# Products of weights and group-norm statistics made beside the scans of a Mamba layer, in a four-layer kernel

## The chip, the core and the metric

The kernel runs on one core of a Trainium2 chip, as one program. The metric is the device time in microseconds (us) of one execution; lower is better. The core has a matrix engine (TensorE, PE in the profile, with its weight loads as PEld), a vector engine (VectorE, DVE), a scalar engine for activations (ScalarE, ACT), a general engine (GpSimd, POOL) and a queue engine that issues nearly all transfers here (SyncE, SP). Each works through its own list of instructions in order; semaphores hold an instruction until what it reads is written and what it overwrites has been read. SBUF is the on-chip memory with 128 partitions (`P`), PSUM the memory that PE writes, in banks of 512 float32 values per partition. DRAM is outside.

## What is computed

Input is `x`, 2 images of 256 channels and 48 x 48 points (`NB` = 2, `C` = 256, `L` = 2304 points), float32. Four layers follow each other:

```python
x = _L0_conv_ref(x, ...)                       # layer 0: Mamba, forward and backward
x = x + _L1_conv_ref(_gn(x), ...)              # layer 1: linear attention, 3x3 conv, MLP
t = _to_tokens(x)
t = t + _L2_attn_ref(_ln_t(t), W_embed, b_embed, W_out, b_out)   # layer 2
t = t + _L2_ffn_ref(_ln_t(t), ...)             # experts gated by a graph
t = t + _L3_attn_ref(_ln_t(t), q_weight)       # layer 3
t = t + _L3_ffn_ref(_ln_t(t), ...)             # mixture of experts
```

Three pieces of it bear on the change.

The group norm between layers 0 and 1, over groups of 8 channels and all points of an image:

```python
g = v.reshape(B_, G, C_ // G, H_, W_)
m = jnp.mean(g, axis=(2, 3, 4), keepdims=True)
s = jnp.var(g, axis=(2, 3, 4), keepdims=True)
return ((g - m) / jnp.sqrt(s + eps)).reshape(v.shape)
```

The scans of layer 0: for every channel of 512 and each of 16 states, h(t) = exp(dt A) h(t-1) + dt u B, y = sum over states of h C, once forward and once backward over the points.

The attention of layer 2, three heads, in which queries, keys and values are consecutive thirds of the points and the head's matrix `W` (768 x 256) and bias `b` serve all three:

```python
e = jnp.einsum('bmc,hc->bmh', x, W) + b
q, k, v = jnp.split(e, 3, axis=1)
attn = jax.nn.softmax(jnp.einsum('bmd,bnd->bmn', q, k) * SCALE, axis=-1)
return jnp.einsum('bmn,bnd->bmd', attn, v)
```

The heads' outputs are concatenated along the points and multiplied by `W_out` (256 x 768), and `b_out` is added.

## The kernel before

The state of the network stays in SBUF between layers: `xres` (residual stream, 128 partitions x 2 halves of the channels x 4608 points) and `xn` (its normalised form). Points are handled in pieces of `W` = 384; an image has `NCH` = 6 pieces. The program is written as Python functions with generators; a scheduler then orders the instructions of each engine, and derives the semaphores from the tiles. Tiles come from pools; a tag with `bufs` = n has n buffers in turn, and a new tile waits until the old content of its buffer has been used.

**Layer 0** (L130 to L434) runs 24 scans, in the order batch, forward then backward, piece (list `order`, L405). In this text a scan's index counts them from 0. One scan covers one piece of 384 points and has 4 blocks of channels x 16 states = 64 operations. Each operation is: an exponential on ACT (L376), a scan instruction on DVE (L382 forward, L385 backward), a product with C on DVE or POOL (L390, tile `hc`; 40 of the 64 on DVE, 24 on POOL), and a product with the identity on PE that sums into `yp` (L344). POOL also makes the products dt u B (`db`, L359, four states at a time). B and C rows are loaded by SP, spread over all partitions (`bb`, `cc`), four states at a time, from two buffers each.

Beside a scan, other work is advanced in small steps: `scan` takes a list `beside` of (generator, number of steps, end) and, after every second operation, calls the generators so that their steps are spread evenly until slot `end` of 32 (L395 to L399). Beside go `project_out` of the scan before (2 steps, backward scans only; it adds into `xres`), `prepare` of the next scan (15 steps: convolution L266, projections L282 and L296, several activations), and, in scans 0 to 9, `project_in` of a later piece (12 steps; layer norm L176 to L195 and 8 products of two matmuls, L202, each copied by ACT and stored by SP). All this work takes its PSUM tile from `hold()`: while scans run, that is one bank, pool `ps` with one buffer, tag "mm". The other PSUM banks hold the exponentials (pool `psh`, five) and `yp` (two). `prepare`'s products are therefore made and evicted one at a time. `pos`, `h`, `sq` and `rs` are single-buffered tiles of `project_in`.

At the start of layer 0 SP loads the small constants, the first piece of `xres`, the projection weights `w_in` (1 MB, L154), the position table, and the other pieces of `xres`.

**Layer 1** (L459 to L675) first loads its weights, makes two block matrices with `same_block` (`gmat`, which averages over groups of 8 channels, and `hmask`), clears the padded image `img` on POOL (L500), and calls `group_norm(0)`: 12 `bn_stats`, two aggregates, a product with `gmat` that averages the means over a group (L520), some small operations, a second one for the variances (L528), root and reciprocal, then `xn` = (x - mean) / sigma in two instructions (L533). Then come keys and values (`pk`, L547), which read `xn`. `group_norm(1)` is called within batch 0's pieces. A part of the sort of the graph's edges (helpers around L880 to L910) is spread over layer 1 and reaches into layer 2.

**Layer 2's attention** (L680 to L816) uses that W embeds queries and keys alike: q k' = x (W' W) x', and the values' path is `W_out` W. Both products depend on weights alone. For each of three heads, `W_embed[h]` and `W_outT` are loaded side by side into `w_eo` (two transfers of 768 KB, L708 and L709), and `gm[h]` = W'[W, W_out'] is made in two blocks of 128 rows, each of six matmuls 128x512 (L713), copied by DVE (L717). The bias terms `ub` are matmuls with one column (L721), 24 per head. Then, per batch, `xv` is made by transposing `xn` (L741, L742), and for each head queries `pq` (L750) from `gm` and `xn`, scores `sp` (L764), softmax, output and the residual.

The records of float32 matmuls in the profile come in pairs: one matmul of the program is two records.

Of the kernel before, what the change touches and what calls it, by code (L numbers as in the profile page):

```python
# [52 lines left out]
class Env:  # L53


    def __init__(self, ctx, tc, p):
# [16 lines left out]
        self.xres = const.tile([P, 2, T], F32, name="xres")  # L73

    def uid(self):
        self.n_pools += 1
        return self.n_pools
# [37 lines left out]
def run(steps):  # L115
    for _ in steps:
        pass


# [9 lines left out]
def layer0(ctx, E):  # L129
# [33 lines left out]
    def hold():  # L163

        pool, tag = (ps, "mm") if scanning else (psh, "hs")
        return pool.tile([P, W], F32, tag=tag, name="mm")

    def project_in(b, c):
# [13 lines left out]
        for k in range(2):  # L182
            nc.tensor.matmul(vp, lhsT=E.mean_c, rhs=sq[:, k, :], start=k == 0, stop=k == 1)
        rs = up.tile([P, W], F32, tag="rs", name="rs")
        nc.scalar.activation(rs, vp, AF.Sqrt, bias=E.eps[1e-5])
# [132 lines left out]
    def project_out(b, c, y):  # L318

        for m in range(2):  # L320
# [8 lines left out]
            yield  # L329

    def scan(step, beside, b, s, c, xs, y, dt, dtu, bcd):

# [19 lines left out]
        for d0, g in [(d0, g) for d0 in range(0, DB, 2) for g in range(NS // GN)]:  # L352
# [4 lines left out]
            for d in (d0, d0 + 1):  # L357
# [14 lines left out]
                for j in range(GN):  # L372
                    n = g * GN + j
                    on_pool = j in GP[(g + d) % 2]
                    hs = psh.tile([P, W], F32, tag="hs", name="hs")
                    nc.scalar.activation(  # L376
# [46 lines left out]
    pieces = [(0, c) for c in range(2, NCH)] + [(1, c) for c in range(NCH)]  # L423
    after = None
    for i, (b, s, step, c) in enumerate(order):
        now, ready = ready, []
        beside = [(after, 2, 5)] if after else []
        if i + 1 < len(order):
            nb, s2, _, c2 = order[i + 1]
            beside.append((prepare(nb, s2, c2, ready), 15, 25))  # L430
        if i < len(pieces):
            beside.append((project_in(*pieces[i]), 12, 32))
        scan(step, beside, *now)
        after = project_out(b, c, now[4]) if s == "b" else None  # L434
# [25 lines left out]
def layer1(ctx, E, edges):  # L460
# [20 lines left out]

    gmat = big.tile([P, P], F32, name="gmat")
    same_block(E, lw, gmat, 3, 1.0 / 8)
    hmask = big.tile([P, P], F32, name="hmask")
# [25 lines left out]
    def group_norm(b):  # L510

        xb = E.xres[:, :, b * L : (b + 1) * L]
        mv = wp.tile([P, 2, 2], F32, tag="mv", name="mv")
        for k in range(2):
            st = wp.tile([P, NCH, 6], F32, tag="st", name="st")
            for c in range(NCH):
                nc.vector.bn_stats(st[:, c, :], xb[:, k, c * W : (c + 1) * W])
            nc.vector.bn_aggr(mv[:, k, :], st)
        pg = ps.tile([P, 2], F32, tag="mm", name="pg")
        nc.tensor.matmul(pg, lhsT=gmat, rhs=mv[:, :, 0], start=True, stop=True)  # L520
        gm = wp.tile([P, 2], F32, tag="gm", name="gm")
        nc.vector.tensor_copy(gm, pg)
        dv = wp.tile([P, 2], F32, tag="dv", name="dv")
        nc.vector.tensor_tensor(dv, mv[:, :, 0], gm, ALU.subtract)
        nc.vector.tensor_tensor(dv, dv, dv, ALU.mult)
        nc.vector.tensor_tensor(dv, dv, mv[:, :, 1], ALU.add)
        gv = ps.tile([P, 2], F32, tag="mm", name="gv")
        nc.tensor.matmul(gv, lhsT=gmat, rhs=dv, start=True, stop=True)  # L528
        gr = wp.tile([P, 2], F32, tag="gr", name="gr")
        nc.scalar.activation(gr, gv, AF.Sqrt, bias=E.eps[1e-5])  # L530
        nc.vector.reciprocal(gr, gr)
        for k in range(2):
            nc.vector.tensor_scalar(  # L533
                E.xn[:, k, b * L : (b + 1) * L], xb[:, k, :], gm[:, k : k + 1], gr[:, k : k + 1],
                ALU.subtract, ALU.mult,
            )
# [150 lines left out]
def layer2_attn(ctx, E):  # L687

    nc, tc, p = E.nc, E.tc, E.p
    NH, D = 3, 768
    S = L // NH
    DT, ST, HW2 = D // P, S // P, S // 2
# [4 lines left out]
    ub = big.tile([P, NH, 4], F32, name="ub")  # L700
    with (
        tc.tile_pool(name="l2wt", bufs=2) as wts,
        tc.tile_pool(name="l2wps", bufs=2, space=PSUM) as ps,
    ):
        for h in range(NH):

            w_eo = wts.tile([P, DT, 2 * C], F32, tag="w_eo", name="w_eo")
            nc.sync.dma_start(w_eo[:, :, 0:C], p["W_embed"][h].rearrange("(k p) m -> p k m", p=P))  # L708
            nc.sync.dma_start(w_eo[:, :, C:], p["W_outT"].rearrange("(k p) m -> p k m", p=P))  # L709
            for m in range(2):  # L710
                pg = ps.tile([P, 2 * C], F32, tag="pg", name="pg")
                for k in range(DT):
                    nc.tensor.matmul(  # L713
                        pg, lhsT=w_eo[:, k, m * P : (m + 1) * P], rhs=w_eo[:, k, :],
                        start=k == 0, stop=k == DT - 1,
                    )
                nc.vector.tensor_copy(gm[:, h, m, :], pg)  # L717
            pu = ps.tile([P, 4], F32, tag="pu", name="pu")
            for m in range(4):
                for k in range(DT):  # L720
                    nc.tensor.matmul(  # L721
                        pu[:, m : m + 1], lhsT=w_eo[:, k, m * P : (m + 1) * P],
                        rhs=E.v("b_embed", h * DT + k, 1), start=k == 0, stop=k == DT - 1,
                    )
            nc.vector.tensor_copy(ub[:, h, 0:2], pu[:, 0:2])
            nc.vector.tensor_tensor(ub[:, h, 2:4], pu[:, 2:4], E.v("b_out"), ALU.add)

# [6 lines left out]
    for b in range(NB):  # L734
# [8 lines left out]
        for h in range(NH):  # L743
            qq = act.tile([P, 2, S], F32, tag="qq", name="qq")
            for m in range(2):
                for g in range(2):
                    gs = slice(g * HW2, (g + 1) * HW2)
                    pq = ps.tile([P, HW2], F32, tag="mm", name="pq")
                    for k in range(2):
                        nc.tensor.matmul(  # L750
                            pq, lhsT=gm[:, h, k, m * P : (m + 1) * P],
                            rhs=xn[:, k, t0 + g * HW2 : t0 + (g + 1) * HW2], start=k == 0, stop=k == 1,
                        )
                    nc.scalar.activation(qq[:, m, gs], pq, AF.Identity, bias=ub[:, h, m : m + 1])

# [45 lines left out]
            for m in range(2):  # L801
                for g in range(2):
                    o = t0 + h * S + g * HW2
                    py = ps.tile([P, HW2], F32, tag="mm", name="py")
                    for k in range(2):
# [5 lines left out]
                    nc.vector.scalar_tensor_tensor(  # L811
                        y, py, ub[:, h, 2 + m : 3 + m], xn[:, m, o : o + HW2], ALU.add, ALU.add
                    )
# [838 lines left out]
def layer3_attn(E, gate, psl):  # L1652
# [313 lines left out]
```

## Time and profile before

| | |
|---|---|
| time of the runs, median (lowest to highest of 3) | 5448.44 us (5447.45 to 5450.56) |
| the profiled execution's own time | 5416.49 us |
| its span, first to last instruction | 5414.7 us |
| instructions | 47212 |
| busy PE / DVE / ACT / POOL, share of the span | 88% / 65% / 44% / 45% |
| layer 0, end of the last addition to `xres` | about 2399 us |
| layer 1, end of its last product on PE | about 3111.6 us |
| layer 2's first product on data (`pq`) | 3181.60 us |

Times inside a trace count from the span's start. The profiled execution is 32 us shorter than the median of the runs; 1.8 us of it lie outside its span. "Busy" is the time in which an engine executes an instruction; register, branch, semaphore and DMA-issuing instructions are not counted. In the slices each digit is the busy share of a 40th of the span in tenths. `PEclk` is the clock granted to PE, in tenths of full speed. In the timeline a row is a run of like instructions: start, length, engine, line, operation, written tile and read tiles, shape, count, and in brackets how long the engine was idle before and what ended that.

The two costliest lines of layer 0 as the page groups them (line, engine, operation, count, then busy us and mean ns of one, then idle time before and its main releaser):

```profile
L359 POOL TENSOR_TENSOR db<-dtu,bb 128x1536 f32<-128x1536 f32 x384 | 1332.3, 3471 | 49.7 <-issue 19.1
L344 PE MATMUL yp<-hc,ident 128*128 128x384 f32 x3072 | 1203.1, 525 | 291.6 <-DVE hc L390 251.7
```

### The profile page before, as it was taken

To read this page: it belongs to the slowest core of one execution; us is meant where nothing else is said; L and a number is where in the kernel's file an instruction comes from. 1 tells how busy PE (TensorE), PEld (TensorE's weight loads), DVE (VectorE), ACT (ScalarE), POOL (GpSimd) and SP (SyncE) were. 2 spreads that over 40 slices of the span, in tenths; PEclk is the share of its full clock that TensorE was granted. 3 is DMA by queue.
4 is the path that set the end of the run, shared out by engine and by line. 5 is a ranking of instruction groups with operands and counts; after the bars stand their busy time and mean duration, and the time that the engine had idled before them with its cause. 6 is when DMAs were issued, how large, how long until landed. Compare 5 with 4: busy or idle time off the path is not lost. (4 is left out here: it accounts for less than half of the span.)

```text
span 5414.7 us, 47212 instructions
## 1 busy us (share of the span) xinstructions
PE 4771.7 (88%) x15246; PEld 2653.7 (49%) x15246; DVE 3503.3 (65%) x5360; ACT 2365.8 (44%) x4935; POOL 2410.2 (45%) x1308
## 2 busy tenths in 40 slices
PE   7888888888877778769999999999999999999897
PEld 3444444443333334335555555556654455555675
DVE  4899898898999898899996234447634401212343
ACT  5767777666667666632222213332123222222111
POOL 3888887788999888860000000008802100000321
PEclk8999999999999889989999989999999999999898
DMA  4445454443545444431110010011122200000422
GB/s 162 163 170 179 161 177 171 156 150 140 172 148 178 152 152 158 146 138 33 40 38 6 0 39 0 27 36 30 22 71 55 61 3 9 6 9 8 84 82 93
DMA packets 178083, 491.28 MB, mean 91 GB/s; under 512 B 32182, under 2 KB 100666, under 8 KB 177562
## 3 DMA queue, kind: packets, MB, share of 16 engines
q1 hardware_dynamic: 169114, 475.36, 25.6%
q0 software_dynamic: 8704, 12.73, 1.6%
q8 instruction: 124, 2.03, 0.2%
q14 instruction: 141, 1.16, 0.1%
HBM read 416.44 MB, written 71.58 MB: 90 GB/s over the span
## 5 line engine op out<-in xcount | busy, mean ns | idle before, releaser
L344 PE MATMUL yp<-hc,ident 128*128 128x384 f32 x3072 | 1203.1, 525 | 291.6 <-DVE hc L390 251.7
L359 POOL TENSOR_TENSOR db<-dtu,bb 128x1536 f32<-128x1536 f32 x384 | 1332.3, 3471 | 49.7 <-issue 19.1
L344 PEld LDWEIGHTS yp<-hc,ident 128*128 128x128 f32 x3072 | 577.1, 199 | 873.5 <-DVE hc L390 447.6
L390 POOL TENSOR_TENSOR hc<-ho,cc 128x384 f32<-128x384 f32 x576 | 579.4, 1014 | 185.3 <-DVE ho L382 83.3
L390 DVE TENSOR_TENSOR hc<-hs,cc 128x384 f32<-128x384 f32 x960 | 498.5, 540 | 39.1 <-PE yp L344 37.8
L376 ACT ACTIVATE hs<-dt,negab 128x384 f32<-128x384 f32 x768 | 434.2, 581 | 93.3 <-DVE ho L385 42.1
L376 ACT ACTIVATE hs<-dt,negaf 128x384 f32<-128x384 f32 x768 | 433.4, 581 | 55.0 <-DVE hc L390 25.5
L385 DVE TENSOR_TENSOR_SCAN hs<-hs,state,db 128x384 f32<-128x384 f32 x400 | 395.1, 1010 | 56.0 <-POOL db L359 30.3
L382 DVE TENSOR_TENSOR_SCAN hs<-hs,state,db 128x384 f32<-128x384 f32 x400 | 396.1, 1010 | 30.2 <-POOL db L359 22.9
L1771 POOL DMA_INDIRECT xe<-xt_d,token x48 | 47.4, 987 | 754.3 <-issue 716.0
L266 PE MATMUL mm<-xw,w_cv 128*128 128x384 f32 x768 | 287.5, 510 | 67.2 <-ACT xs L270 29.4
L1706 PE MATMUL po<-at,xtok 128*128 128x384 f32 x864 | 329.9, 507 | 7.7 <-ACT at L1704 7.5
L912 POOL PARTITION_ALL_REDUCE most<-most x1 | 0.4, 380 | 738.6 <-DVE most L911 738.6
L1697 PE MATMUL sp<-qT,xn 128*128 128x384 f32 x864 | 317.4, 487 | 0.0
L1704 ACT ACTIVATE at<-sp 128x384 f32<-128x384 f32 x216 | 104.6, 490 | 472.7 <-PE sp L1697 472.6
L1354 PE MATMUL ph<-xn,w 128*128 128x384 f32 x768 | 288.2, 519 | 19.3 <-ACT hid L1358 7.6
L627 PE MATMUL pf<-t,wfc 128*128 128x384 f32 x768 | 255.5, 489 | 0.0
L646 PE MATMUL po<-hid,wfc 128*128 128x384 f32 x768 | 253.6, 486 | 0.0
L385 DVE TENSOR_TENSOR_SCAN ho<-hs,state,db 128x384 f32<-128x384 f32 x240 | 240.0, 1000 | 15.2 <-ACT hs L376 15.1
L382 DVE TENSOR_TENSOR_SCAN ho<-hs,state,db 128x384 f32<-128x384 f32 x240 | 239.5, 998 | 8.4 <-ACT hs L376 8.2
L266 PEld LDWEIGHTS mm<-xw,w_cv 128*128 128x128 f32 x768 | 145.9, 196 | 195.1 <-ACT xs L270 46.9
L392 ACT COPY state<-hs 128x1 f32<-128x1 f32 x800 | 117.5, 155 | 278.2 <-DVE hc L390 276.3
(433 smaller groups left out, 7947.6 us busy)
## 6 DMA issues: line engine op xcount, KB each, us to landing
bb<-bcd SPq DMA_DIRECT2D x192, 768.0 KB, 4.1
cc<-bcd SPq DMA_DIRECT2D x192, 768.0 KB, 4.1
xw<-xi_d SPq DMA_DIRECT2D x24, 774.0 KB, 5.3
w<-in_m_w SPq DMA_DIRECT2D x16, 1024.0 KB, 5.8
y_d<-y SPq DMA_DIRECT2D x32, 384.0 KB, 2.3
ye<-y_d SPq DMA_DIRECT2D x32, 384.0 KB, 3.5
xi_d<-xz SPq DMA_DIRECT2D x48, 192.0 KB, 3.0
z_d<-xz SPq DMA_DIRECT2D x48, 192.0 KB, 3.2
```

The lines of the kernel that those rows point to most:

```text
L266: nc.tensor.matmul(px, lhsT=w_cv[b, s][:, d * 4 + k, :], rhs=xw[:, d, o : o + W], start=k == 0, stop=k == 3,)
L344: nc.tensor.matmul(yp[d], lhsT=E.ident, rhs=hc, start=False, stop=summed[d] == NS)
L359: nc.gpsimd.tensor_tensor(db, bc(dtu[:, d, :], [P, GN, W], 1), bb, ALU.mult)
L376: nc.scalar.activation(hs, dt[:, d, :], AF.Exp, scale=nega[s][:, d * NS + n : d * NS + n + 1])
L382: nc.vector.tensor_tensor_scan(to, hs, db[:, j], init, ALU.mult, ALU.add)
L385: nc.vector.tensor_tensor_scan(to[:, ::-1], hs[:, ::-1], db[:, j, ::-1], init, ALU.mult, ALU.add)
L390: (nc.gpsimd if on_pool else nc.vector).tensor_tensor(hc, to, cc[:, j, :], ALU.mult)
L627: nc.tensor.matmul(pf, lhsT=wfc1[:, k, f * P : (f + 1) * P], rhs=t1[:, k, :], start=k == 0, stop=k == 1,)
L646: nc.tensor.matmul(po[m], lhsT=wfc2[:, f, m * P : (m + 1) * P], rhs=hid[:, i, :], start=f == 0, stop=f == 15,)
L1354: nc.tensor.matmul(ph, lhsT=w1[:, e, k, f * P : (f + 1) * P], rhs=xn[:, k, c * W : (c + 1) * W], start=k == 0, stop=k == 1,)
L1697: nc.tensor.matmul(sp, lhsT=xn[:, k, t0 + i * P : t0 + (i + 1) * P], rhs=qT[:, k, c * W : (c + 1) * W], start=k == 0, stop=k == 1,)
L1706: nc.tensor.matmul(po[m], lhsT=xtok[:, i, m * P : (m + 1) * P], rhs=at, start=i == 0, stop=i == MT - 1,)
```

## The change

Two pieces of work are taken out of the seams between layers and put beside layer 0's scans.

- **Head products.** A generator `head_products` in layer 0 makes layer 2's products in 12 rounds of 3 steps: head (3) x block of rows (2) x half of the 768 inner rows (2, `z`). A round loads 3 x 128 rows of `W_embed[h]` and `W_outT` (six transfers of 128 KB) into the tiles `pos`, `h` and `sq` of `project_in`; makes 3 matmuls 128x512 into the bank "mm"; for `z` = 0 ACT copies the result into `part` (the tile `rs`, widened to 512), for `z` = 1 DVE adds the second half to `part` and SP stores it to `gm_d` in DRAM; then 6 matmuls of one column for the bias terms, copied or added by DVE into `ub`. Scans 10 to 21, in which `project_in` has ended, take one round each. Layer 2 now only loads `gm` from `gm_d`, three transfers of 512 KB.
- **Statistics of batch 0.** `group_stats`, taken out of `group_norm`, is a generator of 15 steps and runs beside scan 13, the second forward scan of batch 1, when batch 0's `xres` is complete. Its results stay in `E.gn`. Layer 1 calls it for batch 1 as before, and `group_norm` keeps the two instructions that write `xn`.
- For both, `gmat` moves from layer 1 to the start of the program (a pool `envw`, which is closed again, lends it scratch memory), `gn` and `ub` become constants, `gm_d` is added, and the tiles from `hold()` and the `hs` tiles are declared 512 wide, which is the whole bank that they had anyway.
- In layer 3, the first normalisation takes its tiles from a pool of its own with one buffer (`l3ln1`) instead of `lw`.

```diff
@@ Env.__init__
         self.xres = const.tile([P, 2, T], F32, name="xres")
+
+        self.gmat = const.tile([P, P], F32, name="gmat")
+        with tc.tile_pool(name="envw", bufs=1) as wp:
+            same_block(self, wp, self.gmat, 3, 1.0 / 8)
+        self.gn = const.tile([P, NB, 2, 2], F32, name="gn")
+
+        self.gm_d = self.dram.tile([3, 2, P, 2 * C], F32, name="gm_d")
+        self.ub = const.tile([P, 3, 2, 2], F32, name="ub")
@@ new function
+def group_stats(E, wp, bank, b):
+    nc = E.nc
+    xb = E.xres[:, :, b * L : (b + 1) * L]
+    gm, gr = E.gn[:, b, 0], E.gn[:, b, 1]
+    mv = wp.tile([P, 2, 2], F32, tag="mv", name="mv")
+    for k in range(2):
+        st = wp.tile([P, NCH, 6], F32, tag="st", name="st")
+        for c in range(NCH):
+            nc.vector.bn_stats(st[:, c, :], xb[:, k, c * W : (c + 1) * W])
+            yield
+        nc.vector.bn_aggr(mv[:, k, :], st)
+    pg = bank()
+    nc.tensor.matmul(pg, lhsT=E.gmat, rhs=mv[:, :, 0], start=True, stop=True)
+    nc.vector.tensor_copy(gm, pg)
+    yield
+    dv = wp.tile([P, 2], F32, tag="dv", name="dv")
+    nc.vector.tensor_tensor(dv, mv[:, :, 0], gm, ALU.subtract)
+    nc.vector.tensor_tensor(dv, dv, dv, ALU.mult)
+    nc.vector.tensor_tensor(dv, dv, mv[:, :, 1], ALU.add)
+    gv = bank()
+    nc.tensor.matmul(gv, lhsT=E.gmat, rhs=dv, start=True, stop=True)
+    nc.scalar.activation(gr, gv, AF.Sqrt, bias=E.eps[1e-5])
+    yield
+    nc.vector.reciprocal(gr, gr)
+    yield
@@ layer0
     def hold():
         pool, tag = (ps, "mm") if scanning else (psh, "hs")
-        return pool.tile([P, W], F32, tag=tag, name="mm")
+        return pool.tile([P, 512], F32, tag=tag, name="mm")[:, :W]
...
-        rs = up.tile([P, W], F32, tag="rs", name="rs")
+        rs = up.tile([P, 2 * C], F32, tag="rs", name="rs")[:, :W]
...
+    def head_products():
+        DT, D = 6, 768
+        for h, m, z in [(h, m, z) for h in range(3) for m in range(2) for z in range(2)]:
+            w_eo = []
+            for k in range(3):
+                rows = slice((z * 3 + k) * P, (z * 3 + k + 1) * P)
+                t = up.tile([P, 2, W], F32, tag=("pos", "h", "sq")[k], name="w_eo")
+                t = t.rearrange("p k w -> p (k w)")[:, : 2 * C]
+                nc.sync.dma_start(t[:, 0:C], p["W_embed"][h, rows, :])
+                nc.sync.dma_start(t[:, C:], p["W_outT"][rows, :])
+                w_eo.append(t)
+            yield
+            pg = ps.tile([P, 2 * C], F32, tag="mm", name="pg")
+            for k in range(3):
+                nc.tensor.matmul(
+                    pg, lhsT=w_eo[k][:, m * P : (m + 1) * P], rhs=w_eo[k], start=k == 0, stop=k == 2
+                )
+            if z == 0:
+                part = up.tile([P, 2 * C], F32, tag="rs", name="part")
+                nc.scalar.copy(part, pg)
+            else:
+                nc.vector.tensor_tensor(part, part, pg, ALU.add)
+                nc.sync.dma_start(E.gm_d[h, m], part)
+            yield
+            pu = ps.tile([P, 2 * C], F32, tag="mm", name="pu")
...
+            ub = E.ub[:, h, m, :]
+            if z == 0:
+                nc.vector.tensor_copy(ub, pu[:, 0:2])
+            else:
+                nc.vector.tensor_tensor(ub, ub, pu[:, 0:2], ALU.add)
+                nc.vector.tensor_tensor(ub[:, 1:2], ub[:, 1:2], E.v("b_out", m, 1), ALU.add)
+            yield
...
         if i < len(pieces):
             beside.append((project_in(*pieces[i]), 12, 32))
+        elif i < len(pieces) + 12:
+            beside.append((islice(heads, 3), 3, 32))
+        if (b, s, step) == (1, "f", 1):
+            beside.append((group_stats(E, up, lambda: hold()[:, 0:2], 0), 15, 32))
         scan(step, beside, *now)
@@ layer1
-    gmat = big.tile([P, P], F32, name="gmat")
-    same_block(E, lw, gmat, 3, 1.0 / 8)
...
     def group_norm(b):
-
+        if b:
+            run(group_stats(E, wp, lambda: ps.tile([P, 2], F32, tag="mm", name="pg"), b))
...
@@ layer2_attn
-        for h in range(NH):
-
-            w_eo = wts.tile([P, DT, 2 * C], F32, tag="w_eo", name="w_eo")
...
+    ub = E.ub
+    for h in range(NH):
+        nc.sync.dma_start(gm[:, h], E.gm_d[h].rearrange("m p c -> p m c"))
@@ layer3
+        tc.tile_pool(name="l3ln1", bufs=1) as ln1,
...
-        behind = normalize_piece(E, lw, psl, T // W - 1)
+        behind = normalize_piece(E, ln1, psl, T // W - 1)
```

More of the change, by code (lines that the diff above doesn't have):

```diff
@@ L8 @@
 from contextlib import ExitStack
-from itertools import chain
+from itertools import chain, islice
 import numpy as np
@@ L329, in project_out @@
             yield
+    def head_products():
[23 more added lines that the diff above has]
+            pu = ps.tile([P, 2 * C], F32, tag="mm", name="pu")
+            for i in range(2):
+                o = i * C + m * P
+                for k in range(3):
+                    nc.tensor.matmul(
+                        pu[:, i : i + 1], lhsT=w_eo[k][:, o : o + P],
+                        rhs=E.v("b_embed", h * DT + z * 3 + k, 1), start=k == 0, stop=k == 2,
+                    )
+            ub = E.ub[:, h, m, :]
[5 more added lines that the diff above has]
+            yield
     def scan(step, beside, b, s, c, xs, y, dt, dtu, bcd):
@@ L374, in scan @@
                     on_pool = j in GP[(g + d) % 2]
-                    hs = psh.tile([P, W], F32, tag="hs", name="hs")
+                    hs = psh.tile([P, 512], F32, tag="hs", name="hs")[:, :W]
                     nc.scalar.activation(
@@ L424, in layer0 @@
     after = None
+    heads = head_products()
     for i, (b, s, step, c) in enumerate(order):
@@ L510, in group_norm @@
     def group_norm(b):
+        if b:
+            run(group_stats(E, wp, lambda: ps.tile([P, 2], F32, tag="mm", name="pg"), b))
         xb = E.xres[:, :, b * L : (b + 1) * L]
[L513 to L531, printed above, removed]
         for k in range(2):
             nc.vector.tensor_scalar(
-                E.xn[:, k, b * L : (b + 1) * L], xb[:, k, :], gm[:, k : k + 1], gr[:, k : k + 1],
-                ALU.subtract, ALU.mult,
+                E.xn[:, k, b * L : (b + 1) * L], xb[:, k, :], E.gn[:, b, 0, k : k + 1],
+                E.gn[:, b, 1, k : k + 1], ALU.subtract, ALU.mult,
             )
@@ L692, in layer2_attn @@
     nc, tc, p = E.nc, E.tc, E.p
-    NH, D = 3, 768
+    NH = 3
     S = L // NH
-    DT, ST, HW2 = D // P, S // P, S // 2
+    ST, HW2 = S // P, S // 2
     scale = C**-0.5
@@ L699, in layer2_attn @@
     gm = big.tile([P, NH, 2, 2 * C], F32, name="gm")
[L700 to L704, printed above, removed]
-        for h in range(NH):
-            w_eo = wts.tile([P, DT, 2 * C], F32, tag="w_eo", name="w_eo")
[L708 to L726, printed above, removed]
+    ub = E.ub
+    for h in range(NH):
+        nc.sync.dma_start(gm[:, h], E.gm_d[h].rearrange("m p c -> p m c"))
     act = ctx.enter_context(tc.tile_pool(name="l2act", bufs=2))
@@ L753, in layer2_attn @@
                         )
-                    nc.scalar.activation(qq[:, m, gs], pq, AF.Identity, bias=ub[:, h, m : m + 1])
+                    nc.scalar.activation(qq[:, m, gs], pq, AF.Identity, bias=ub[:, h, m, 0:1])
             norms = [normalize_piece(E, wp, psn, (b - 1) * NCH + c) for c in range(2 * h, 2 * h + 2) if b]
@@ L811, in layer2_attn @@
                     nc.vector.scalar_tensor_tensor(
-                        y, py, ub[:, h, 2 + m : 3 + m], xn[:, m, o : o + HW2], ALU.add, ALU.add
+                        y, py, ub[:, h, m, 1:2], xn[:, m, o : o + HW2], ALU.add, ALU.add
                     )
```

## The prediction

> **What bounds the kernel now.** I read the busy slices first, then windows over single scans, then the timeline at the two seams the change touches (layer 0 to 1 and layer 1 to 2), then waits. Slices of the page, each digit a 40th of the span (135 us):
>
> ```profile
> PE   7888888888877778769999999999999999999897
> DVE  4899898898999898899996234447634401212343
> POOL 3888887788999888860000000008802100000321
> PEclk8999999999999889989999989999999999999898
> ```
>
> Until the 18th slice (about 2400 us) DVE runs at 8 to 9 tenths beside PE and POOL at 7 to 9: the 24 scans. Then PE alone is full. So work put on DVE in the scans costs nearly its length; work taken off PE at a seam, where nothing else is queued, is worth nearly its length.
>
> Windows from a scan's first operation to the next scan's (stretch, length, busy us and count of PE, PEld, DVE, ACT, POOL, clock, DMA share, GB/s):
>
> ```profile
> 381.70:478.20 96.50, 79.57 (x224) 39.55 (x224) 89.51 (x113) 69.47 (x169) 83.16 (x42) 1.00 0.49 168
> 1461.30:1551.40 90.10, 71.24 (x185) 32.65 (x184) 86.46 (x109) 61.66 (x154) 82.60 (x42) 0.96 0.46 158
> 1821.40:1925.20 103.80, 72.25 (x165) 33.68 (x166) 83.95 (x111) 64.58 (x153) 82.51 (x42) 0.84 0.44 160
> 2021.50:2117.80 96.30, 75.37 (x209) 38.37 (x208) 85.52 (x114) 64.68 (x153) 81.27 (x42) 0.95 0.43 156
> ```
>
> First a forward scan with project_in beside it, then one without: 6.4 us apart. Below, two backward scans without it; the first (index 18) has a stall of its own, 7.5 us over the second.
>
> Layer 0 to layer 1, and layer 1 to layer 2, by the timeline (start, us, engine, line, operation, count, idle before and its releaser):
>
> ```profile
> 2399.11 4.27 POOL L500 MEMSET img<- 128x5000 f32 x1
> 2399.22 4.24 DVE L852 CAST lo_row<-iota 128x128 f32<-128x128 int32 x1
> 2399.56 3.90 DVE L517 BATCH_NORM_STATS2 st<-xres 128x6 f32<-128x384 f32 x1
> 2408.44 1.93 DVE L517 BATCH_NORM_STATS2 st<-xres 128x6 f32<-128x384 f32 x4
> 2415.65 2.85 DVE L533 TENSOR_SCALAR xn<-xres,gm,gr 128x2304 f32<-128x2304 f32 x2
> 2417.16 1.22 PE L547 MATMUL pk<-wqkv,xn 128*128 128x512 f32 x1 [2.44 <-DVE xn L533]
> ...
> 3112.93 0.38 SPq L708 DMA_DIRECT2D w_eo<-in_W_embed  x1
> 3118.14 5.25 PE L721 MATMUL pu<-vec,w_eo 128*128 128x1 f32 x24 [2.50 <-DMA w_eo<-in_W_embed]
> 3178.72 0.15 DVE L726 TENSOR_TENSOR ub<-pu,vec 128x2 f32<-128x2 f32 x1
> 3179.01 2.79 PE L741 MATMUL tp<-ident,xn 128*128 128x128 f32 x12 [0.41 <-DVE ub L726]
> 3181.60 6.38 PE L750 MATMUL pq<-xn,gm 128*128 128x384 f32 x16
> ```
>
> At the first seam layer 1's first product pk waits until 2417.16 for the statistics of batch 0. At the second, PE works from 3118 to 3179 on products of weights that need no data of the run; the first product of layer 2 on data is pq at 3181.60.
>
> **Layer 1 to layer 2: -55 us.** Removed are the rows of pg and pu (72 and 144 matmul records, 36.5 and 23.5 us) and the wait for w_eo. In their place three loads of gm, 512 KB each, stand where w_eo's first stood (3112.93; it landed after 5.2 us), so gm is there by about 3118. In the changed order PE runs tp, ln_mean, tp, ln_var, tp, pq, and the fourth xv copy, whose bank pq takes, stands on DVE behind the last normalisation's reciprocal: half-sum ends 3118.4, ln_var and its root about 3120.0, reciprocal 2.55, one MAX8 0.43, the xn product 0.96, one replace 0.41, the copy 0.43: 3124.8. So pq moves from 3181.6 to 3124.8, -57. The rest of the edge sort (five pairs of MAX8 and replace of 0.84, then 2) now runs ahead of layer 2's first maximum rather than under the products, and may hold it: I take back 2. The Trainium skill ("TensorE: Matmul & The Clock Gate", What's actually happening) speaks of a second cost: PE falls to half its clock after an idle window of about 3.4 us and needs as long, busy, to recover. The rows show it (pk's first takes 1.22 us after 12.7 us without a product), and PE will idle for some 6 us here too. By the rule pq's first matmuls would take 1.7 us longer; but in the trace of before pq's first weight loads stand 0.63 us apart (3182.28, 3182.91) and the later twelve 0.32, so PE was at half clock there as well: the cost is in both kernels, and I add nothing. Bounds -45 (gm lands after 10 us, the sort in front) to -58.
>
> **Layer 0 to layer 1: -10.5 us.** 12 bn_stats (0.48 pitch, from the row x4 in 1.93), two aggregates, the two small matmuls and their chain go, and gmat with them. What is late next? The memset of img, 4.27 us on POOL. The Trainium skill ("SBUF — State Buffer", Who interferes with whom) calls the port pair that DVE shares with GpSimd an exclusive lock. The rows agree: the CAST and the bn_stats that start 0.1 and 0.45 us after the memset last 4.24 and 3.90 and end with it, at 2403.4, where a bn_stats takes 0.5 elsewhere. The memset stays, so xn starts at 2403.4: 1.46 + 0.42 for mask and reciprocals + 1.46 gives pk at 2406.7, against 2417.2. Without the lock xn would end near 2403 and pk would wait only for wqkv (landed 2403.59), a gain of 13.6. I take the rows: -10.5 (-8 to -13).
>
> **Head products beside scans 10 to 21: +18 us.** Each of 12 scans gets six loads of 128 KB, 3 matmuls of 128x512 (6 records at 0.43 pitch, 2.6 us), 6 of one column (12 records, 2.6 us), and evictions. DVE: every other scan one copy of 0.16; the others an add from PSUM, priced by the 128x512 copy of 0.69, and two of 0.15; mean 0.58. PE has 19 to 21 us free per scan, so 5.2 us fit if they do not hold yp back. The nearest row is project_in beside a scan: 6.5 to 8 us longer, of which DVE's own rows (0.95 + 2.55 + 0.96 + 1.15) make 5.6; the residual 1 to 2.4 is the price of 12.3 PE us, 8 ACT copies and 10 turns of the one bank. For 5.2 PE us and 2 turns that is 0.4 to 1.0. I take 1.5 per scan, a little over 0.58 + 0.7, because the next instruction on PE after pg is a dt product (L296) that needs the same bank: it waits for pg's eviction, and yp queues behind it. In scans 11, 19 and 21 the add stands behind up to eight scan operations (1.0 each) on DVE. Range +6 to +36 (0.5 to 3 per scan). The loads add 0.75 MB to some 15 MB per scan, at 0.43 to 0.49 of the DMA engines: hidden; uncovered they would be about 2 us per scan at the 390 GB/s seen at the start. Six more issues on SP per scan, 0.4 to 0.5 each, stand between bb and cc loads that are issued two groups ahead.
>
> **Statistics in the scans: +8 us.** 12 x 0.48 + 2 x 0.30 + five small DVE rows of 0.14 to 0.16 make 7.1; they are on DVE, which is the bound there, and the scheduler has spread them over scans 8 to 13. Two more table loads (1.28 each, around one Sqrt) fall on ACT in scan 13, which is 67% busy: about 1. Range 5 to 12.
>
> **Start: +4 us.** gmat's scratch stands in memory that w_in uses, so the 1 MB load of w_in, third on SP's queue at 1.67, now comes behind pos and five pieces of xres and waits for gmat, built after h: about 9.9. With 4.7 to 5.8 to land it is there at 15 to 16, before its first use (17.60), but everything behind it on SP, six pieces of xres, edges, small weights, then the first xz stores (21.74 now), shifts by some 5 us, and xz has two buffers. Bounds 0 to 7.
>
> **Scan 18: -5 us.** Its excess is one wait in front of yp (9.7 us, DVE hc on PE yp), PE having the next scan's L282 and four L296 ahead of yp. In the changed order these L296 are spread between yp. Bounds -8 to +3 (the jam could appear in another scan).
>
> Layer 3's one-buffer pool for its first normalisation changes no row I can find there: 0.
>
> **Sum**: -55 - 10.5 + 18 + 8 + 4 - 5 = -40.5. The profiled execution took 5416.5 us (span 5414.7), so it would be 5376; the median of the runs is 32 us (0.6%) higher, and I carry the difference over to it: 5448.4 - 40.5 = **5408**.
>
> **Rivals.**
> - A, the one bank (slower side). pg and pu sit in the bank through which the next scan's preparation passes; if PE stalls there, yp is late, hc runs out of its four buffers and DVE stops. The other parts sum to -58.5, so it decides from 4.9 us per head scan. If a head step costs what a project_in step does, 6.5, the sum is +19.5: 5468. For it: yp already delays hc by 37.8 us over the scans, and scan 18 shows that such a jam costs 7.5. Against: PE is idle a fifth of each scan and there are two turns against ten.
> - B, the scans hide all but DVE's rows: 7 for heads, 7 for the statistics, nothing at the start: -56.5, 5392. For it: PE and ACT slack; against: project_in's residual.
> - C, layer 2 starts later: gm's loads wait for layer 1's last readers and land like the later w_eo's (up to 11 us), and the sort's pairs hold the xv copies: +12, so 5420. For it: both queues show this order; against: w_eo's first load had the same release.
>
> **Numbers.** Forecast 0.62, B 0.14, C 0.13, A 0.11 (about half of it slower). Two executions' medians can be told apart from about 0.2%, 11 us: faster by more 0.88, within 0.06, slower 0.06. Best ends sum to -67 (5381), worst to +5 (5453); 8 in 10 lie in 5388 to 5432.
>
> **What would show it.** pq within 13 us of layer 1's last po; pk 7 to 8 us after the last xres add; scans 10 to 21 longer by 1 to 2 us (index 18 shorter); bn_stats rows of 0.5 inside scans 8 to 12; xz stores 2 to 5 us later at the start. It is wrong if head scans grow by 5 us or more with waits of hc on yp, or if pq waits for gm beyond 3130.

## The result, and the profile after

The changed kernel took 5422.04 us (median of 5 runs, 5420.41 to 5425.96) against 5448.44 before (median of 5, 5447.26 to 5457.15). The medians are 26.4 us apart; the ratio on record, over the runs taken beside each other, is 0.994 with a 95% interval of 0.9929 to 0.995, which is 27 to 39 us. The changed kernel is faster, by less than the 40.5 us that were forecast, and inside the stated range.

The two profiled executions seem to contradict that: the span is 5418.6 us after and 5414.7 before. Both kernels have a stage, the graph-gated experts of layer 2, that takes 794 to 797 us in some profiles and 830 to 838 in others. As far as these runs show it goes with the chip: on two chips all eight profiles were of the long kind, on a third both were of the short; on which chip the first two profiles were taken is not on record. The first profile of before is of the short kind, and its timed runs, 32 us over it, are not. Stages must therefore be compared one by one, or profile with profile of the same kind.

Slices of the page after:

```profile
PE   7888888888787778879999989999799999999897
DVE  4999888898999888899996244546534401212343
```

The scans still end in the 18th slice with DVE at 8 to 9. The new 7 in PE's row (29th slice, about 3793 to 3929 us) is the long kind of that stage; the change does not touch it.

Windows of four scans after (index 3, 14, 18 and 20; columns as in the prediction):

```profile
386.07:482.57 96.50, 79.56 (x224) 39.47 (x224) 89.50 (x113) 69.48 (x169) 83.19 (x42) 1.00 0.49 168
1477.18:1568.42 91.24, 75.42 (x222) 38.10 (x220) 82.69 (x109) 64.14 (x160) 81.05 (x42) 1.00 0.49 165
1842.21:1941.69 99.48, 72.84 (x197) 35.69 (x198) 80.63 (x112) 62.87 (x153) 81.04 (x42) 0.93 0.50 175
2042.55:2144.89 102.34, 86.34 (x228) 43.41 (x227) 86.36 (x116) 65.62 (x155) 81.44 (x42) 0.90 0.44 155
```

A scan without new work is the same to 0.01 us (96.50). Index 14 pays 1.2 us for its head step, index 18 lost 4.3 us of its old stall, and index 20 pays 6.0: its DVE is busy 0.8 us longer than before, its PE 8.1 to 11.0 us longer (75.37 in the first profile of before, 78.20 in the second).

The two seams after, by the timeline:

```profile
2431.74 0.38 SPq L556 DMA_DIRECT2D wqkv<-in_Wqkv  x1
2432.01 4.27 POOL L582 MEMSET img<- 128x5000 f32 x1
2432.45 5.10 DVE L597 TENSOR_SCALAR xn<-xres,gn 128x2304 f32<-128x2304 f32 x1
2437.74 1.45 DVE L597 TENSOR_SCALAR xn<-xres,gn 128x2304 f32<-128x2304 f32 x1
2438.43 2.90 PE L611 MATMUL pk<-wqkv,xn 128*128 128x512 f32 x3 [6.82 <-DMA wproj<-in_Wproj]
...
3131.94 0.82 PE L782 MATMUL tp<-ident,xn 128*128 128x128 f32 x6
3133.45 1.40 SPq L767 DMA_DIRECT2D gm<-gm_d  x3
3141.10 2.55 DVE L118 RECIPROCAL ln_rs<-ln_rs 128x384 f32<-128x384 f32 x1 [0.96 <-ACT ln_rs L117]
3145.11 0.41 DVE L783 COPY xv<-tp 128x256 f32<-128x256 f32 x1
3145.62 8.00 PE L791 MATMUL pq<-xn,gm 128*128 128x384 f32 x16 [4.32 <-issue]
```

At the first, the statistics are gone and pk comes 16.1 us after the last scan operation begins (27.5 before). At the second, pq comes 13.5 us after layer 1's last product (70.0 before), right behind the xv copy that starts at 3145.11 (its length, 0.41, ends at 3145.52).

Stage by stage, two pairs of profiles of like kind: before with the changed kernel run again (both short in the experts), and a second profile of before with the first one after (both long):

| stage, us | forecast | short pair | long pair |
|---|---|---|---|
| start, to the first scan operation | +4 | +2.3 | +2.9 |
| first to last scan operation | +21 | +28.0 | +31.6 |
| last scan operation to pk | -10.5 | -11.4 | -11.4 |
| pk to layer 1's last product | 0 | -0.7 | +1.2 |
| to pq | -55 | -56.5 | -53.4 |
| pq to the experts' first product | 0 | +2.2 | +3.6 |
| to the end | 0 | -5.0 | +4.3 |
| sum (span) | -40.5 | -41.1 | -21.2 |

In the last row the change touches only the pool of layer 3's first normalisation. From the graph experts' last `ph<-xn,w` to the end the changed kernel and its variants take 1104.0 to 1110.4 us and the kernel before 1106.2 and 1108.8, so this pool shows no effect, and the row shows how far single profiles scatter. The gain of the runs lies between the two sums.

### The profile page after: what moved, and what is told of

Its sections match the earlier page's. It is cut to its first block, busy times and chain, and to the rows that moved or that the text cites. A ratio compares the mean times of both kernels' runs of the same rounds, so it can differ in the third digit from the quotient of the medians.

```text
span 5418.6 us, 47326 instructions
## 1 busy us (share of the span) xinstructions
PE 4773.2 (88%) x15246; PEld 2642.9 (49%) x15246; DVE 3503.3 (65%) x5372; ACT 2370.0 (44%) x4939; POOL 2403.7 (44%) x1308
## 5 line engine op out<-in xcount | busy, mean ns | idle before, releaser
L1399 ACT ACTIVATE hid<-ph,vec 128x384 f32<-128x384 f32 x192 | 110.6, 581 | 337.2 <-PE ph L1395 244.6
L470 ACT COPY state<-hs 128x1 f32<-128x1 f32 x800 | 117.7, 155 | 293.6 <-DVE hc L468 291.7
```

## The experiments

**The kernel before, again.** No edit.

> The kernel before once more, for a second profile. Theory S: its usual executions (5448 us) hold a stall of some 32 us in layer 2's experts, near the graph's gathers, that the first profiled execution (5416 us) lacked; then this profile has a span near 5447 us, the same times as the first profile until about 3850 us within 1 us, and then a gap of 30 to 35 us on PE, ACT and DVE together. Theory N: the stall is new in the changed kernel; then the extra 32 us of the usual executions lie elsewhere (spread over the stages, or in layer 0), and no such gap is here.

Measured: one run, span 5439.8 us, 5441.66 in all. Theory S holds in what it was about: PE stands for 32.4 us in the experts. Ahead of them the times are not those of the first profile within 1 us, but up to 8.2 us earlier (the experts' first `ph` at 3503.8 against 3512.0). The same place in the first profile after, PE and ACT by the timeline:

```profile
3844.37 0.58 ACT L1399 ACTIVATE hid<-ph,vec 128x384 f32<-128x384 f32 x1 [0.84 <-PE ph L1395]
3849.98 1.21 PE L1410 MATMUL po<-hid,w 128*128 128x384 f32 x3 [0.86 <-issue]
3883.73 0.58 ACT L1399 ACTIVATE hid<-ph,vec 128x384 f32<-128x384 f32 x1 [38.78 <-remote]
3884.36 2.29 PE L1410 MATMUL po<-hid,w 128*128 128x384 f32 x3 [33.17 <-ACT hid L1399]
```

ACT and DVE wait for something that the profile ties to no instruction of the core ("remote") while POOL issues gathers, until some 7 us after the last gather's issue (3877.13). From its first `ph<-xn,w` to its last the stage takes 829.8 us here and 793.9 in the first profile. So the 32 us by which the runs of before exceed its profile lie in one stage, and are not a scale of 0.6%.

**Statistics alone.** The head products are left in layer 2.

```diff
-        elif i < len(pieces) + 12:
-            beside.append((islice(heads, 3), 3, 32))
```

> Statistics and gmat moved as in the change, the head products left in layer 2 as before. If the parts add: start +4.5, statistics in scans 8 to 13 +8, pk earlier against the scans' end by 11.7: within 3 us of before (5446 to 5452). If the statistics collide with the head step of scan 13 in the changed kernel, scan 13 is here under 95 us (97.0 there, 89.4 before) and the sum is a gain of 3 to 6.

Measured: ratio 0.9989 (0.9982 to 0.9996), 5448.29 us, 2 to 10 us faster. The scheduler set one bn_stats each into scans 7 to 11 and seven, with both aggregates, into scan 12. Scan 11 grew by 0.5 us, scan 12 by 1.2 for some 4.3 of DVE's time, scan 13, with the small products and the root, by 3.0; scans 7 to 10 did not grow, and scan 15 shrank by 2: in all 0 to 3.4 us over the scans (2290.3 against 2290.3 and 2286.9 in the two profiles of before), where 8 were forecast. pk came 15.2 us after the last scan operation. Scan 13 was 92.4 us, under 95. Heads alone, the next run, have 93.0 there: of the 7.6 us by which scan 13 grew in the changed kernel, 1.0 belongs to both steps together.

**Heads alone.** The group norm of batch 0 and gmat go back into layer 1.

```diff
-            beside.append((group_stats(E, up, lambda: hold()[:, 0:2], 0), 15, 32))
...
+    same_block(E, lw, E.gmat, 3, 1.0 / 8)
...
-        if b:
+        if True:
```

> Head products beside the scans as in the change; gmat and the statistics of batch 0 left in layer 1, so the start is as before. Theory of the sum: pq -57, scans 10 to 21 +22 to +25, nothing at the start: 5448 - 33 = 5412 to 5418. If the heads cost in the scans only what DVE does for them (7 us): near 5400.

Measured: 5417.12 us, ratio 0.9935 (0.9917 to 0.9954), as by the theory of the sum; pq 13.5 us after layer 1's last product. The scans took 2308.0 us in all, 17.7 to 21.1 over before: about +22 to +26 for the head steps of the other eleven scans and -4.7 in scan 18. The parts do not add up in the scans: by the first profile of before 17.7 and 0 apart, 28.2 together; by the second 21.1 and 3.4, and 31.6. Scan 10 (99.2 against 97.6 with heads alone) and scan 20 (102.3 against 99.0) hold 4.9 of the 7 to 10 us that are missing.

**Late heads.** The same products, but each scan's step comes after the last dt product of the preparation.

```diff
+    def late(steps):
+        next(steps)
+        for _ in range(13):
+            yield
+        next(steps)
+        yield
+        yield
+        next(steps)
+        yield
...
-            beside.append((islice(heads, 3), 3, 32))
+            beside.append((late(heads), 16, 32))
```

> As changed, but each scan's head products come after the last dt product of the next scan's preparation instead of before the first. Theory bank: the cost in scans 19 to 21 (+4.5, +6.0, +6.3 against before) comes from the dt product that waits for pg's eviction in the one bank, after which PE runs at half clock and yp is late; then scans 19 to 21 come down to 97 to 98 us each and the time is 5405 to 5412. Theory work: the scans pay for PE's and DVE's extra instructions wherever these stand; then scans 19 to 21 stay at 100.9 to 102.5 us and the time stays within 3 us of 5422.

Measured: 5402.09 us, ratio 0.9909 (0.9891 to 0.9926). Windows of its scans 19 to 21:

```profile
1937.28:2034.53 97.25, 83.36 (x230) 42.99 (x229) 87.01 (x117) 64.24 (x154) 80.95 (x42) 0.91 0.49 166
2034.53:2130.54 96.01, 80.92 (x227) 42.06 (x226) 85.64 (x115) 65.02 (x154) 81.16 (x42) 0.95 0.46 165
2130.54:2228.14 97.60, 82.42 (x226) 42.66 (x225) 87.00 (x118) 64.72 (x154) 81.20 (x42) 0.91 0.44 157
```

The same work costs -0.3 to +1.4 us per scan here, where it cost 4.6 to 6.3 as changed (against 96.3; scan 19 alone cost 3.3 in the second profile of the changed kernel): theory bank. Only scan 18 keeps more of its old stall than as changed, 102.5 us against 99.5. How it went in the changed kernel, scan 20, by the timeline:

```profile
2086.39 2.84 PE L383 MATMUL pg<-w_eo 128*128 128x512 f32 x6 [0.94 <-ACT pr L322]
2089.07 1.45 PE L422 MATMUL yp<-hc,ident 128*128 128x384 f32 x4
2091.27 0.58 ACT L454 ACTIVATE hs<-dt,negab 128x384 f32<-128x384 f32 x1
2091.79 0.57 ACT L388 COPY part<-pg 128x512 f32<-128x512 f32 x1
2092.41 1.35 PE L332 MATMUL mm<-pr,w_dtb 16*128 16x384 f32 x2 [1.90 <-ACT part L388]
2093.69 4.21 PE L422 MATMUL yp<-hc,ident 128*128 128x384 f32 x6
2096.66 0.56 DVE L468 TENSOR_TENSOR hc<-hs,cc 128x384 f32<-128x384 f32 x1 [1.39 <-PE yp L422]
```

pg is ready at about 2089.2, but its copy stands on ACT behind exponentials and the small copies of states (L470), which wait for DVE's scans, so the bank comes free at 2092.4. PE stands for 1.9 us, and then six yp records take 4.21 us where four took 1.45 before: 0.70 each against 0.36. The clock granted to PE shows why, in two stretches of this scan (columns as in the other windows):

```profile
2089.34:2092.75 3.41, 1.51 (x5) 0.67 (x4) 3.41 (x4) 1.87 (x5) 3.41 (x3) 1.00 0.32 92
2092.75:2102.99 10.24, 10.24 (x16) 4.20 (x14) 6.27 (x11) 5.30 (x15) 6.62 (x4) 0.50 0.34 124
```

PE was busy for 1.51 of 3.41 us, and then its clock was 0.50 for 10.24 us. That is the half clock of "TensorE: Matmul & The Clock Gate" in the Trainium skill (What's actually happening), after a shorter pause than its idle window of some 3.4 us; and it lasted three times the busy window of some 3.4 us that the page gives for the recovery, although the profile counts PE as busy all through it. The waits of this scan, DVE on PE, then PE on the copy (us in all, times, longest):

```profile
DVE hc L468 <- PE yp L422: 5.6, 6, 1.4
...
PE mm L332 <- ACT part L388: 1.9, 1, 1.9
```

A wait of 1.9 us on PE, which had 20 us to spare, became 5.6 us on DVE, which had none; the same scan of the second profile of before lists neither wait. With late heads PE stands even longer for the same copy in this scan, 3.3 us, but then it is pu that waits there, and DVE waits for yp 2.3 us in all.

**No bank wait.** The products stay in place, and only what the two evictions read is exchanged, so that `gm` does not hold the products.

```diff
-                nc.scalar.copy(part, pg)
+                nc.scalar.copy(part, w_eo[0])
...
-                nc.vector.tensor_tensor(part, part, pg, ALU.add)
+                nc.vector.tensor_tensor(part, part, w_eo[0], ALU.add)
```

> As changed, with every instruction of the head products in number and place, but the copy (ACT) and the add (DVE) that evict pg read a weight tile in SBUF in its place, so gm does not hold the products: the dt product behind pg has no eviction to wait for. Theory bank: the wait, and the slower PE after it, are the cost; scans 19 to 21 come to 97 to 99 us (100.9, 102.3, 102.5 as changed) and the time to 5402 to 5410. Theory position: it is pg and pu in front of yp, six and twelve records in the middle of a scan, that make yp late; then scans 19 to 21 stay over 100 us and the time stays at 5418 to 5425.

Measured: 5409.34 us, ratio 0.9914 (0.9897 to 0.993). Scans 19 to 21:

```profile
1936.38:2036.26 99.88, 81.76 (x227) 41.88 (x226) 88.40 (x118) 65.67 (x154) 82.02 (x42) 0.95 0.46 161
2036.26:2133.67 97.41, 79.81 (x227) 40.48 (x226) 85.67 (x115) 65.09 (x153) 81.33 (x42) 0.96 0.45 163
2133.67:2233.54 99.87, 81.86 (x227) 41.90 (x226) 88.39 (x117) 65.26 (x153) 81.84 (x42) 0.95 0.42 153
```

Scan 20, whose eviction is ACT's, falls from 102.3 to 97.4, PE's busy time from 86.3 to 79.8, and the clock rises to 0.96: the wait and what follows it were 5 of its 6 us. Scans 19 and 21, with DVE's add, keep 3.6 of their 4.6 and 6.3, more than theory bank allows and less than theory position; their DVE is busy 3 us longer than before. But the edit did more than was meant. The two evictions, no longer tied to pg, did not keep their place, and an add of two tiles in SBUF took longer than one from PSUM. The add of scan 19 as changed and here, and the copy for scan 20, which now runs in scan 19:

```profile
1991.02 0.67 DVE L390 TENSOR_TENSOR part<-part,pg 128x512 f32<-128x512 f32 x1
...
1962.12 2.54 DVE L390 TENSOR_TENSOR part<-part,w_eo 128x512 f32<-128x512 f32 x1
2015.05 0.62 ACT L388 COPY part<-w_eo 128x512 f32<-128x512 f32 x1
```

Up to 1.9 of the 3.6 us that scans 19 and 21 keep are thus the exchanged operand's own. Over all scans 13.2 us go although the six adds are 7.4 us longer in all; with late heads 17.2 go. So the wait is the larger part of what the place costs; whether it is all of it, this run cannot say.

**Border only.** Layer 1 clears the edge of its image instead of the whole.

```diff
-    nc.gpsimd.memset(img, 0.0)
+    for r in (0, HH + 1):
+        nc.gpsimd.memset(img[:, :, r, :], 0.0)
+    for w in (0, WW + 1):
+        nc.gpsimd.memset(img[:, :, 1 : HH + 1, w], 0.0)
```

> As changed, but layer 1 clears only the border of its padded image, in four small memsets, since the interior is written later in full. Theory lock: the 4.3 us memset on POOL holds DVE's CAST, compare and xn; without it pk comes 2.5 to 3.5 us sooner after the last scan operation (16.0 us as changed), 12.5 to 13.5. Theory DMA: pk waits for wqkv's landing anyway; then it stays at 15 to 16.

Measured: one run, 5419.11 us; by its timeline:

```profile
2428.50 0.38 SPq L556 DMA_DIRECT2D wqkv<-in_Wqkv  x1
2428.77 0.30 POOL L583 MEMSET img<- 128x100 f32 x2
2428.88 0.27 DVE L896 CAST lo_row<-iota 128x128 f32<-128x128 int32 x1
2429.21 1.55 DVE L600 TENSOR_SCALAR xn<-xres,gn 128x2304 f32<-128x2304 f32 x1
2435.32 2.90 PE L614 MATMUL pk<-wqkv,xn 128*128 128x512 f32 x3 [6.95 <-DMA wproj<-in_Wproj]
```

Both halves of the question are answered. Without the long memset the CAST takes 0.27 us and not 4.24, the first xn 1.55 and not 5.10: the lock is real. (Whether it held each of them, or the CAST alone with the others behind it in DVE's order, the rows do not tell.) Yet pk comes 16.1 us after the last scan operation, as with the memset. The packets of wqkv, known by their size of 3072 bytes, end at 2434.49 here and at 2437.60 in the changed kernel, each time 0.83 us ahead of pk. Theory DMA: with the statistics gone, the load ends last, and the lock lies under it, though only just: in the changed kernel the first xn ends at 2437.55, 0.05 us ahead of the load. In two other runs, statistics alone and statistics beside scan 22, the load ended some 1 us ahead of xn; there pk followed xn by 0.2 us and came 15.2 us after the last scan operation.

**Statistics beside scan 22, with late heads.**

```diff
-        if (b, s, step) == (1, "f", 1):
+        if (b, s, step) == (1, "b", 4):
```

> Late head products, and the chain of the statistics beside scan 22, which has no head step, instead of 13. If head step and statistics disturb each other in scan 13 (97.2 us there with late heads, 89.4 before): scan 13 falls to 91 to 92, scan 22 grows from 96.3 to 98 to 100, in all 2 to 3 us less than late heads alone. If the statistics cost their DVE time wherever they are: the same time within 1.5 us in the scans.

Measured: 5403.15 us; scan 13 fell to 92.4, scan 22 rose to 99.5, and the scans took 2300.9 us against 2301.3. The chain costs its 3 to 5 us in either place, as the second theory had it.

**Late heads, border, and scratch of its own** (gmat's scratch in the pool of constants, so that w_in is third on SP's queue again).

```diff
-        with tc.tile_pool(name="envw", bufs=1) as wp:
-            same_block(self, wp, self.gmat, 3, 1.0 / 8)
+        same_block(self, const, self.gmat, 3, 1.0 / 8)
```

> Late head products, border memsets, and gmat's scratch in memory of its own so that w_in is loaded third again. Against late heads alone (5402): 3 us less at the seam to layer 1 by theory lock, and at the start 1 to 4 us less if the moved w_in load costs what the first two profiles differ by (99.4 and 103.9), nothing if that is the scatter of the start (100.9 in the second profile of before): 5395 to 5400.

Measured: 5401.92 us, as late heads alone and not the 5395 to 5400 expected; pk 15.3 us after the last scan operation, the first scan at 102.5 (101.7 with late heads). Neither edit is worth a time that these runs can tell.

**The last normalisation behind pq**, added to the three edits above.

```diff
-    run(normalize_piece(E, lw, psn, NB * NCH - 1))
...
+            if (b, h) == (0, 0):
+                norms = [normalize_piece(E, wp, psn, NB * NCH - 1), iter((0, 0, 0))]
```

> Late head products, border memsets, scratch of its own, and layer 1's last normalisation (the last piece of batch 1, which layer 2 needs only for batch 1) made within the first head of layer 2 instead of before it. As changed, pq waits 13.5 us after layer 1's last product, because the xv copies stand behind that normalisation's reciprocal on DVE. If that is the chain, pq comes 7 to 9 us after it, when gm has landed, and the time is 3 to 7 us under the 5402 of the late versions. If gm's load is what ends last, pq stays at 12 us or more and nothing is gained.

Measured: ratio 0.9896 (0.988 to 0.9913), the lowest of all, though its interval overlaps those of the other late versions; 5351.84 us against 5409.84 of before and 5374.41 of the changed kernel on that chip, where the experts' stage is short. The seam by its timeline:

```profile
3108.68 1.40 SPq L779 DMA_DIRECT2D gm<-gm_d  x3
3113.20 0.41 DVE L795 COPY xv<-tp 128x256 f32<-128x256 f32 x1
3113.71 6.41 PE L803 MATMUL pq<-xn,gm 128*128 128x384 f32 x16
```

pq starts 6.4 us after layer 1's last product, 5.0 after gm's loads were issued, and its 16 records take 6.41 us instead of 8.00. Of the 7 us, 3.7 are paid back in the first head, where the normalisation now runs (pq to the experts 336.2 us against 332.6): some 3 us are left, within the scatter against the other late versions.

**The changed kernel, again.**

> The changed kernel once more, on the chip and beside the runs of before of this call: 5416 to 5428. If the start costs what the first pair of profiles shows, its first scan begins at 103 to 105 us again (103.9); if that was scatter of the first loads, between 100 and 104.

Measured: 5374.41 us, ratio 0.9939 (0.9923 to 0.9956), so the times expected did not hold and the ratio did: this chip has the short experts, for before as well (5409.84). The first scan began at 101.7. Over all profiles here it begins at 101.0 on average in the five where w_in is loaded third (99.4 to 102.5) and at 102.4 in the seven where it is loaded later (101.2 to 103.9): a cost of 1 to 2 us in a scatter of 3.

## Why the prediction held, and where it was off

- **Layer 1 to layer 2** was right step by step: pq 13.5 us after the last product where the working gave 13.2, with the fourth xv copy ending last. gm had landed, its last packet at 3139.89. What was left at nothing, the clock, costs 1.6 to 2.4 us: pq's 16 records take 8.00 us and not 6.38 (5.59 in the second profile of before). Both start at half clock, but after the change PE stays in it longer: 5.26 us into pq against 2.08 (0.50 in the second profile of before). The 1.7 us that the prediction had estimated and then dropped were about right in size. One of its readings was loose: pk's slow first product before the change came 2.44 us after another product; the 12.7 us without one stand ahead of the first small product of the statistics (2411.39), and the clock was 0.50 from 2402.02 to 2422.50.
- **Layer 0 to layer 1** was right in size (-11.4 for -10.5) and wrong in its last step, so the size is in part luck. "What is late next?" was answered by the memset and the lock; the border experiment shows the load of wqkv there. I had taken its landing from the trace of before (4.7 us after issue) and ruled it out; after the change its packets end 5.9 us after issue (4.4 before), and the lock costs nothing. The working also let pk wait for both halves of xn; in the trace it starts while the second is being written (2437.74 to 2439.19), so its path through the lock was about 1.9 us too long, which stood in for the later load.
- **Head products in the scans** were the term mis-sized. The prediction put 1.5 us on each head step from project_in's residual, +18 for twelve, and heads alone show +22 to +26 for the eleven apart from scan 18. It had named the place, the dt product that needs the bank right after pg, and priced it by the work that shares it; a stall of PE must be priced by what queues behind it. Here that is yp, slowed further because PE is left at half clock, and 5.6 us of DVE's time in scan 20. Rival A was thus the mechanism, at about a third of its price of 6.5 per step, which is why the sum kept its sign. The prediction's own sign of being wrong, head scans that grow by 5 us or more with hc waiting for yp, did show in scans 20 (6.0 us more, 5.6 us of such waits) and 21 (6.3 and 6.0); the others grew by less, but for scan 13, which has the statistics as well.
- **Statistics**: alone 0 to 3.4 us, not 8. The twelve bn_stats, priced at their full DVE time, cost 1.7 (scans 11 and 12): they fill gaps. Beside the heads the two cost 7 to 10 more than apart; why scans 10 and 20 differ between the two kernels was not tried further.
- **Scan 18**: -4.3 to -4.7 for -5. **Start**: +1 to +2 over all profiles, +2.3 and +2.9 in the two pairs, for +4.
- **From profile to median**: carrying 32 us over as a share of 0.6% was wrong in kind, though it did no harm. They lie in the experts' stage alone, 830 us against 794.

The forecast of 40.5 is met by the short pair (-41.1) because the scans' 7 us too many stand against small gains elsewhere, 5.0 of them scatter in the last row of the table, where nothing was forecast: that match is luck. The runs say 27 to 39.

## What to carry to other kernels

A product slipped in beside a full pipeline costs little for its work and much for its place: look which instruction next needs its PSUM bank, on which engine its eviction queues, and behind what. Here moving the same products 21 to 33 us later in their scan (45 in scan 13) was worth 17 us, about half of what the whole change had brought. When a wait is removed at a seam, list every load that was issued there too, with its landing after the change rather than before.

## What was not expected of the hardware

- PE came out of a pause of 1.9 us at half rate (yp at 0.70 us a record, 0.36 ahead of it), and its clock stayed at 0.50 for 10.24 us: two dt records take 1.35 at 2092.41, and 0.91 again at 2103.30. It need not stand still to lose its clock. In every trace here the clock changes lie whole multiples of 3.41 us apart. Cutting the trace of the changed kernel into such stretches gives 1350 at full clock that full clock followed, and PE was busy for at least 42% of each; of the 62 falls to half, 51 follow a stretch in which it was busy for 52% or less. The other 11 fit no such limit.
- With gathers being issued by POOL, ACT and DVE stood for up to 40 and 50 us without a releaser on the core, in executions on some chips and not on others, in both kernels. In the first profile after, instruction packets on queue 14 arrive at 3882.05, 2 us after the last gather packet, and the engines go on at 3883.7; in the second profile of before they arrive at 3904.78, 2 us after the last gather packet at 3902.9. That the engines waited for instructions held up behind the gathers would fit, and was not tested. The gap on PE varied from 13 to 33 us while the stage took 830 to 838 us in each of these, so the gap alone is not its price.
